# Transposes in row groups: a decoder layer's self attention on one NeuronCore

## The chip, the cores and the metric

The kernel runs on one core of one Trainium2 chip. The metric is the device time of one execution in microseconds (us), the median of several runs. The engines are called PE (TensorE; its weight loads are listed apart, as PEld), DVE (VectorE), ACT (ScalarE), POOL (GpSimd) and SP (SyncE, which issues the DMAs).

## The reference

One encoder layer over a short context (2 sequences of 77 rows) and one decoder layer over 2 sequences of T = 2048 rows, D = 512 wide, H = 16 heads of 32, all in float32. Cut to its core:

```python
def _mha(xq, xkv, w_in, b_in, w_out, b_out, bias):
    ...
    scores = jnp.einsum('bhqd,bhkd->bhqk', q, k) / jnp.sqrt(jnp.asarray(hd, xq.dtype))
    attn = jax.nn.softmax(scores + bias[None], axis=-1)
    out = jnp.einsum('bhqk,bhkd->bhqd', attn, v)
    return out.transpose(0, 2, 1, 3).reshape(Bq, Tq, D) @ w_out.T + b_out
...
x = x + _mha(_ln(x, ...), _ln(x, ...), enc_in_w, ...)          # encoder
memory = x + (relu(_ln(x, ...) @ enc_ff1_w.T + enc_ff1_b) @ enc_ff2_w.T + enc_ff2_b)
yn = _ln(y, dec_n1_s, dec_n1_b)
y = y + _mha(yn, yn, dec_sa_in_w, ..., sb)                     # causal, with a table of biases
y = y + _mha(_ln(y, ...), memory, dec_ca_in_w, ..., cb)
y = y + (relu(_ln(y, ...) @ dec_ff1_w.T + dec_ff1_b) @ dec_ff2_w.T + dec_ff2_b)
```

## The kernel before

**Stages.** The rows of x are cut into blocks of 512: two sequences b, four blocks m each. First comes self attention for all eight blocks; the small encoder runs in its first block, and the cross attention of the first block (`first_cross`) in the gaps of the second sequence. Then a second phase does cross attention and the feed-forward layer of each block, with products of halves and quarters (L1323, L1352, L1424) after Strassen's scheme.

**Self attention.** A unit is 128 query rows (t) of a block and a head group g of four heads: 128 units, each with i+1 = 4m+t+1 chunks of 128 keys. `pieces` cuts the chunks into pieces of one to four (kn). For each piece `scores` makes four matmuls, one for each head r, of 32 rows each on the four row groups of PE, into four PSUM banks (L376). DVE moves them to `pp` with their maxima (L385; the last 256 columns of a unit are added to the bias on the way, L392), and makes the negative maximum once the unit's scores are all there (L402). ACT makes the exponentials (L407), four a unit, put into the program bit by bit by `exps`.

`turn` takes one or two pieces, transposes the probabilities chunk by chunk and head by head (128 x 128, L428), four to a bank, and copies each filled bank to `pts` (L434 on ACT, L432 on DVE). For m = 0 the copies alternate between the engines; else the first half of the loads goes to ACT and the second to DVE. `values` then multiplies `pts` by the values, four heads side by side in columns, into bank 7 (L445).

**Order.** It is written out by hand (a manual schedule): every engine runs its instructions in the order in which the Python code emits them. The loop at the end takes one or two pieces of a unit and emits `turn`, then, after the unit's last piece, `slot` (a projection q, k, v or out, L215, L226, L239, L251; the turning of a normed row tile in `norm_turn`, L308; the division by the sums in `divide`, L464), one group of scores if `may_score` allows it, the values, and further scores. With m = 3 each unit has two turns of two pieces, of which the second has the projection; with m = 2 one of two pieces and one of one; with m = 1 one of two; with m = 0 one of one piece.

**Banks.** In self attention `bank()` hands out seven PSUM banks in a ring: four for a group of scores, one for each load of four transposes, one for a projection. In the second phase the ring has four. The buffer `pts` has room for 32 transposed tiles of 128 x 128, as many as a turn of two whole pieces makes.

**Second phase.** `norm_stages` turns a normed tile with four transposes into one bank (L759) and four activations. `attend_stages` turns the probabilities over the 77 context rows, four heads to a bank (L814), and copies each with ACT (L815).

Of the kernel before, what the change touches and what calls it, by code (L numbers as in the profile page):

```python
# [11 lines left out]
AF = mybir.ActivationFunctionType  # L12
ALU = mybir.AluOpType
# [41 lines left out]
def tile_encoder_decoder(ctx: ExitStack, tc: tile.TileContext, ins, out):  # L55
    nc = tc.nc
    x, src = ins["x"], ins["ctx_1024"]
# [10 lines left out]
    ident = const.tile([P, P], F32, name="ident")  # L68
# [89 lines left out]
    with (  # L158
# [6 lines left out]
        kT = ac.tile([P, NC, T], F32, name="kT")  # L165
# [28 lines left out]
        nTs, qTs, ots, sums_of = {}, {}, {}, {}  # L194
        wbig, xs, xr = {}, {}, {}
# [102 lines left out]
        def norm_turn(b, m, t, apart=False):  # L298
            xn = xs.pop((b, m, t))
            if t == 0:  # L300
                nTs[b, m] = nTt
            nT = nTs[b, m]

            pts = [bank()] * NC
            if apart:
                pts[0] = bank()
            for c in range(NC):
                nc.tensor.transpose(pts[c][:, ts(c, P)], xn[:, ts(c, P)], ident)  # L308
            for c in range(NC):
                d, pt = nT[:, c, ts(t, P)], pts[c]  # L310
                sc, bi = vec("dec_n1_s", c), vec("dec_n1_b", c)
                if c or not apart:
                    nc.scalar.activation(d, pt[:, ts(c, P)], AF.Identity, bias=bi, scale=sc)  # L313
                else:
                    nc.vector.tensor_scalar(d, pt[:, ts(c, P)], sc, bi, ALU.mult, ALU.add)


        def pieces(i):
# [94 lines left out]
        def turn(pieces):  # L413

            first = units[pieces[0][0]][1] == 0
            by_head = first or units[pieces[0][0]][2:] == (0, 0)
            loads = []
            for n, k0, kn in pieces:
                ks = range(k0, k0 + kn)
                if by_head:  # L420
                    loads += [[(n, k, r) for k in ks] for r in range(HC)]
                else:
                    loads += [[(n, k, r) for r in range(HC)] for k in ks]
            for o, load in enumerate(loads):
                pt = bank()
                pts = in_turn("pts", pts_all).rearrange("p (x q) -> p x q", q=P)
                for x, (n, k, r) in enumerate(load):
                    nc.tensor.transpose(pt[:, ts(x, P)], state[n]["p"][r][:, ts(k, P)], ident)  # L428
                    got[n, k, r] = pts[:, x, :]
                w = len(load) * P  # L430
                if o % 2 if first else o >= (len(loads) + 1) // 2:
                    nc.vector.tensor_copy(pts[:, : len(load), :], pt[:, :w])  # L432
                else:
                    nc.scalar.copy(pts[:, : len(load), :], pt[:, :w])  # L434
                if o == min(3, len(loads) - 1):
                    exps(1)
            exps(HC if first else 1)

# [14 lines left out]
        def divide(b, m, g):  # L453


            ri = sm.tile([P, TB, HC], F32, name="ri", tag="ri", bufs=2)
            nc.vector.reciprocal(ri, sums_of[b, m, g])
            rows = sm.tile([P, TB, HC, HD], F32, name="rirows", tag="rirows", bufs=1)
            nc.vector.tensor_copy(rows, ri[:, :, :, None].to_broadcast([P, TB, HC, HD]))
            yield  # L460
            rb = bank()
            flat = rows.rearrange("p t r d -> p (t r d)")
            for t in range(TB):
                nc.tensor.transpose(rb[:, ts(t, P)], flat[:, ts(t, P)], ident)  # L464
            nc.vector.tensor_tensor(ots[b, m, g], rb, ots[b, m, g], ALU.mult)
            yield


# [266 lines left out]
        def norm_stages(y, n, row, place, done):  # L735

            keep = {}

            def stats():
                st = sm.tile([P, 6], F32, name="bnst", tag="bnst")  # L740
                mv = sm.tile([P, 2], F32, name="cmv", tag="cmv", bufs=4)
                rs = sm.tile([P, 3], F32, name="crs", tag="crs", bufs=4)
                nc.vector.bn_stats(st, y())
                nc.vector.bn_aggr(mv, st)
                nc.vector.tensor_scalar_add(rs[:, 0:1], mv[:, 1:2], EPS)
                nc.gpsimd.tensor_tensor(rs[:, 1:2], rs[:, 0:1], mhalf[:, 0:1], ALU.pow)
                nc.gpsimd.tensor_scalar(rs[:, 2:3], mv[:, 0:1], rs[:, 1:2], -1.0, ALU.mult, ALU.mult)
                keep.update(rs=rs)

            def center():  # L750
                xn = keep["xn"] = place()
                rs = keep["rs"]
                nc.scalar.activation(xn, y(), AF.Identity, bias=rs[:, 2:3], scale=rs[:, 1:2])
                nc.gpsimd.tensor_tensor(y(), y(), row, ALU.add)

            def turned():
                xn, pt, dst = keep["xn"], bank(), done()
                for c in range(NC):
                    nc.tensor.transpose(pt[:, ts(c, P)], xn[:, ts(c, P)], ident)  # L759
                for c in range(NC):  # L760
                    sc, bi = vec(f"dec_{n}_s", c), vec(f"dec_{n}_b", c)
                    nc.scalar.activation(dst[:, c, :], pt[:, ts(c, P)], AF.Identity, bias=bi, scale=sc)

            return stats, center, turned

# [6 lines left out]
        def attend_stages(q, kTc, v, y, biased, pr, pts, place, w_o, bi=None):  # L772


            prh = pr.rearrange("p (h k) -> p h k", k=S)
# [32 lines left out]
                nc.gpsimd.tensor_tensor(prh, prh, ri[:, :, None].to_broadcast([P, H, S]), ALU.mult)  # L808

            def turned():  # L810
                for g in range(NC):
                    pt = bank()
                    for r in range(HC):
                        nc.tensor.transpose(pt[:S, ts(r, P)], prh[:, g * HC + r, :], ident)  # L814
                    nc.scalar.copy(pts(g), pt[:S, :])  # L815

            def times_v():
                ot = bank()
                for g in range(NC):
                    for r in range(HC):  # L820
                        h = g * HC + r
                        nc.tensor.matmul(  # L822
                            ot[rows4(r), ts(g, P)], v[:, ts(h, HD)], pts(g)[:, ts(r, P)], start=True, stop=True
                        )
                keep["oT"] = place()
                nc.scalar.copy(keep["oT"], ot)
# [9 lines left out]
        def first_cross():  # L836
# [21 lines left out]
            def pts(g):  # L858
                return kT[:S, g, 2 * MB : 3 * MB]

            def loads():
                for t in range(TB):
# [581 lines left out]
        def cross(x):  # L1444
# [26 lines left out]
            for t in range(TB):  # L1471
                at = 14 + 7 * t
                y = lambda t=t: y_of(x, t)
                biased = m == 0 and t < 2
                fs = attend_stages(
                    lambda g, t=t: qT[g // 2][:, g % 2, ts(t, P)], kTcs[b], vcs[b][:S, :], y, biased, pr,
                    lambda g: pts_all[:S, g, :], place("xr"), wbt,
                    bias_1 if biased and t else None,
                )
# [35 lines left out]
        i = 0  # L1515
# [93 lines left out]
```

## Time and profile before

| | |
|---|---|
| Median of 3 runs | 2827.0 us (2826.58 to 2828.27) |
| Span of the profiled execution | 2828.5 us |
| PE busy | 2796.6 us, 99% |
| DVE, ACT, POOL busy | 66%, 51%, 28% |
| Transposes of probabilities, L428 | 4352, busy 536.6 us |
| Their copies | 556 on DVE (L432), 330.8 us; 598 on ACT (L434), 298.8 us |
| Scores, L376 | 2560 instructions (two passes each), busy 356.6 us |
| Values, L445 | 8704 instructions (two passes each), busy 278.8 us |

The profile is of one execution; its span and the median agree within 1.5 us. An engine's busy time is the time in which at least one of its instructions ran, so instructions that overlap count once; the mean is that of one instruction from its start to its end, with the time in the pipeline. The chain of waits starts at the last instruction and goes back, at each step, to what released it. In the views, "<-" after an idle time names what ended it.

### The profile page before, as it was taken

Reading aid. Unit: us, or ns where it says so; the run is one execution under the profiler, and the core shown is the slowest. Engines: PE = TensorE matmul, PEld = TensorE weight load, DVE = VectorE, ACT = ScalarE, POOL = GpSimd, SP = SyncE. Lnnn points to the kernel's source line nnn. Section 1 sums busy time; section 2 is a strip of 40 time slices with the busy share of each in tenths; the row PEclk is TensorE's granted clock in tenths of the full one; section 3 lists DMA queues with packets and bytes.
Section 4 is the critical chain, followed back from the end, with each engine's and each line's share of the span. In section 5 each row is a group of like instructions: output and inputs, shape, how many; then the busy total and the mean of one; then the engine's idle time right before and its main releaser. Section 6 shows DMA issues by size and latency. Waiting matters only on the chain.

```text
span 2828.5 us, 65166 instructions
## 1 busy us (share of the span) xinstructions
PE 2796.6 (99%) x25950; PEld 2062.6 (73%) x25950; DVE 1872.9 (66%) x5288; ACT 1454.0 (51%) x2785; POOL 787.9 (28%) x697
## 2 busy tenths in 40 slices
PE   9899999999999999999999999999999999999998
PEld 5557666666666556666666677888888888888888
DVE  4666687778887577687878895464645555555545
ACT  3544466656666556656656676434344444444431
POOL 0200050200000201120100002282828283837356
PEclk9999999999999999999999999999999999999999
DMA  6414343401111412332401014463637464646466
GB/s 172 122 33 130 119 137 103 125 17 46 34 44 58 120 48 61 80 102 68 124 20 32 21 60 144 135 216 116 205 120 207 138 197 127 194 131 187 125 201 194
DMA packets 252642, 319.10 MB, mean 113 GB/s; under 512 B 29568, under 2 KB 142512, under 8 KB 252210
## 3 DMA queue, kind: packets, MB, share of 16 engines
q1 hardware_dynamic: 252338, 314.93, 37.7%
q8 instruction: 205, 3.36, 0.5%
q14 instruction: 99, 0.81, 0.1%
HBM read 274.91 MB, written 39.95 MB: 111 GB/s over the span
## 4 chain that ended last, share of the span: by engine, by line
PE 93%; DVE 3%; ACT 1%; issue 1%; DMA 1%; POOL 1%; SPq 0%; POOLq 0%; ACTq 0%; DVEq 0%
PE psum L428 17%; PE psum L1323 14%; PE psum L1352 12%; PE psum L376 11%; PE psum L445 9%; PE psum L215 4%; PE psum L831 4%; PE psum L251 4%; PE psum L239 4%; PE psum L226 3%; PE psum L1424 3%; PE psum L814 2%; DVE pp L385 1%; PE psum L784 1%; PE psum L822 1%; PE psum L546 1%
## 5 line engine op out<-in xcount | busy, mean ns | idle before, releaser
L407 ACT ACTIVATE pp<-pp,nm 128x128 f32<-128x128 f32 (+15 forms) x512 | 612.7, 1204 | 219.7 <-DVE nm L402 219.2
L385 DVE TENSOR_SCALAR_CACHE_REDUCE pp<-psum 128x512 f32<-128x512 f32 (+3 forms) x1024 | 559.4, 591 | 61.7 <-PE psum L376 60.2
L428 PEld LDWEIGHTS psum<-ident,pp 128*128 128x128 f32 x4352 | 472.9, 141 | 111.8 <-DVE pp L385 53.1
L428 PE MATMUL psum<-ident,pp 128*128 128x128 f32 x4352 | 536.6, 277 | 9.2 <-ACT pp L407 2.8
L434 ACT COPY pts<-psum 128x512 f32<-128x512 f32 (+3 forms) x598 | 298.8, 571 | 437.6 <-PE psum L428 333.4
L432 DVE COPY pts<-psum 128x512 f32<-128x512 f32 (+3 forms) x556 | 330.8, 648 | 68.6 <-PE psum L428 68.5
L376 PE MATMUL psum<-kT,q 32*128 32x512 f32 (+3 forms) x2560 | 356.6, 576 | 6.0 <-ACT nT L313 2.7
L445 PEld LDWEIGHTS psum<-pts,vv 128*32 128x32 f32 x8704 | 226.0, 110 | 123.9 <-issue 116.0
L1352 PEld LDWEIGHTS psum<-pp 128*128 128x128 f32 x2560 | 295.8, 192 | 17.4 <-issue 12.8
L1352 PE MATMUL psum<-pp 128*128 128x128 f32 x2560 | 306.4, 276 | 1.9 <-POOL pp L1105 1.6
L445 PE MATMUL psum<-pts,vv 128*32 128x128 f32 x8704 | 278.8, 275 | 0.7 <-ACT pts L434 0.5
L1105 POOL TENSOR_TENSOR pp<-pp 128x512 f32<-128x512 f32 x155 | 209.5, 1368 | 111.7 <-DMA pp<-in_dec_ff_wT_dram 90.8
L1323 PE MATMUL psum<-vv,pp 128*128 128x256 f32 x1024 | 238.5, 381 | 0.0
L376 PEld LDWEIGHTS psum<-kT,q 32*128 32x128 f32 x2560 | 122.9, 183 | 141.2 <-issue 87.9
L1323 PEld LDWEIGHTS psum<-vv,pp 128*128 128x128 f32 x1024 | 189.8, 190 | 26.3 <-issue 1.9
L392 DVE CUSTOM_DVE_ANT_0 pp<-psum,bias 128x256 f32<-128x256 f32 (+1 forms) x512 | 196.0, 411 | 17.0 <-PE psum L376 17.0
L285 POOL TENSOR_TENSOR rstd<-rstd,mhalf 128x1 f32<-128x1 f32 x32 | 18.2, 569 | 659.1 <-DVE rstd L284 608.6
L1336 DVE TENSOR_TENSOR kT<-kT,psum 128x512 f32<-128x512 f32 x96 | 65.7, 685 | 181.0 <-PE psum L1323 181.0
L1339 ACT ACTIVATE kT<-kT,vecs 128x256 f32<-128x256 f32 x192 | 86.9, 500 | 168.7 <-DVE kT L1336 168.1
L1323 PE MATMUL psum<-nT,pp 128*128 128x256 f32 x768 | 173.4, 379 | 0.0
L1323 PEld LDWEIGHTS psum<-nT,pp 128*128 128x128 f32 x768 | 145.3, 190 | 22.6 <-issue 3.5
L808 POOL TENSOR_TENSOR oT<-oT,cri 128x1232 f32<-128x1232 f32 x28 | 67.7, 2416 | 283.4 <-DVE cri L803 258.4
(193 smaller groups left out, 3724.5 us busy)
## 6 DMA issues: line engine op xcount, KB each, us to landing
pp<-w_d SPq DMA_DIRECT2D x520, 256.0 KB, 2.9
pp<-in_dec_ff_wT_dram SPq DMA_DIRECT2D x112, 256.0 KB, 4.0
wqk<-in_dec_sa_in_wT_dram SPq DMA_DIRECT2D x64, 256.0 KB, 4.0
bias<-tzg SPq DMA_DIRECT2D x128, 128.0 KB, 3.8
wbig<-in_dec_sa_in_wT_dram SPq DMA_DIRECT2D x8, 1024.0 KB, 6.4
vv<-in_enc_ff_wT_dram SPq DMA_DIRECT2D x8, 1024.0 KB, 5.2
wbig<-in_dec_sa_out_wT_dram SPq DMA_DIRECT2D x8, 1024.0 KB, 6.4
vv<-y SPq DMA_DIRECT2D x32, 256.0 KB, 5.1
```

Source lines behind the costliest of these rows:

```text
L215: nc.tensor.matmul(mm, w[:, c, :], nTs[b, m][:, c, :], start=(c == 0), stop=(c == NC - 1))
L376: nc.tensor.matmul(banks[r][:, : kn * P], q[rows4(r), ts(t, P)], kT[rows4(r), g, k0 * P : (k0 + kn) * P], start=True, stop=True,)
L385: nc.vector.tensor_scalar(p[:, k0 * P : (k0 + far) * P], s[:, : far * P], 1.0, None, ALU.mult, ALU.max, accum_out=st["mx"][:, r, c : c + 1],)
L392: nc.vector.tensor_tensor_reduce(p[:, (i + 1) * P - w : (i + 1) * P], s[:, far * P : kn * P], biases[b, m, g][:, r, 2 * P - w :], 1.0, LOW ...
L407: nc.scalar.activation(p, p, AF.Exp, bias=nm, accum_out=to)
L428: nc.tensor.transpose(pt[:, ts(x, P)], state[n]["p"][r][:, ts(k, P)], ident)
L432: nc.vector.tensor_copy(pts[:, : len(load), :], pt[:, :w])
L434: nc.scalar.copy(pts[:, : len(load), :], pt[:, :w])
L445: nc.tensor.matmul(ot[rows4(r), t, :], vv[:, k, ts(g * HC + r, HD)], got.pop((n, k, r)), start=(k == 0), stop=(k == i),)
L1105: engine.tensor_tensor(out, a, b, ALU.subtract)
L1323: nc.tensor.matmul(mm[:, ts(f, TOK)], a[:, c, ts(f, P)], b[:, c, :], start=fresh and f == 0 and c == 0, stop=c == 1, skip_group_check=True,)
L1352: nc.tensor.matmul(psum[:, bank_i, ts(col, P)], lhs[:, c, :], w[:, c, :], start=fresh and k in (0, 3) and c == 0, stop=c == 3, skip_group_ ...
```

## The change

`turn` makes each 128 x 128 transpose in four parts: 32 query rows each, on the row group of those rows, and each row group writes to a bank of its own. So a piece of kn chunks fills four banks together, each with w = 4 kn strips of 32 columns, and then has four copies: banks 0 and 2 by DVE, 1 and 3 by ACT, in this order of emission DVE, ACT, DVE, ACT. A copy writes runs of 32 columns, 128 apart. `pts` is handed out by tiles instead of by loads of four. The exp that stood after a turn's fourth load stands after its first piece.

The other transposes of 128 rows (`norm_turn`, `divide`, `turned` in `norm_stages` and in `attend_stages`) are made in two parts of 64 rows, into two banks (`two_banks`, `turn_halves`); the instruction that empties them reads both banks at once, or, in `attend_stages`, copies eight heads' strips of one bank for two head groups at a time.

The diff, cut to its core:

```diff
+HALF = P // 2
...
+        pts_ring = pts_all.rearrange("p s (x q) -> p (s x) q", q=P)
...
+        def two_banks():
+            n = count["bank"]
+            count["bank"] += 2
+            i, j = sorted((n % count["banks"], (n + 1) % count["banks"]))
+            return psum[:, i : j + 1 : j - i, :]
+
+        def turn_halves(pt, x, src, width=P):
+            for a in range(2):
+                rows = slice(a * HALF, (a + 1) * HALF)
+                nc.tensor.transpose(pt[:width, a, ts(x, HALF)], src[rows], ident[rows, rows])
+
+        def joined(t):
+            return t.rearrange("p (a q) -> p a q", a=2)
...
-            pts = [bank()] * NC
+            pts = [two_banks()] * NC
...
-                nc.tensor.transpose(pts[c][:, ts(c, P)], xn[:, ts(c, P)], ident)
+                turn_halves(pts[c], c, xn[:, ts(c, P)])
...
         def turn(pieces):
             first = units[pieces[0][0]][1] == 0
-            by_head = first or units[pieces[0][0]][2:] == (0, 0)
-            loads = []
-            for n, k0, kn in pieces:
+            if count["pts"] + sum(HC * kn for _, _, kn in pieces) > pts_ring.shape[1]:
+                count["pts"] = 0
+            for o, (n, k0, kn) in enumerate(pieces):
                 ks = range(k0, k0 + kn)
...
-            for o, load in enumerate(loads):
-                pt = bank()
-                pts = in_turn("pts", pts_all).rearrange("p (x q) -> p x q", q=P)
-                for x, (n, k, r) in enumerate(load):
-                    nc.tensor.transpose(pt[:, ts(x, P)], state[n]["p"][r][:, ts(k, P)], ident)
+                first_unit = first or units[n][2:] == (0, 0)
+                load = [(k, r) for r in range(HC) for k in ks] if first_unit else [(k, r) for k in ks for r in range(HC)]
+                w = len(load)
+                pt = [bank() for _ in range(HC)]
+                pts = pts_ring[:, count["pts"] : count["pts"] + w, :]
+                count["pts"] += w
+                for x, (k, r) in enumerate(load):
+                    for a in range(HC):
+                        rows = rows4(a)
+                        nc.tensor.transpose(
+                            pt[a][:, ts(x, HD)], state[n]["p"][r][rows, ts(k, P)], ident[rows, rows]
+                        )
                     got[n, k, r] = pts[:, x, :]
-                w = len(load) * P
-                if o % 2 if first else o >= (len(loads) + 1) // 2:
-                    nc.vector.tensor_copy(pts[:, : len(load), :], pt[:, :w])
-                else:
-                    nc.scalar.copy(pts[:, : len(load), :], pt[:, :w])
-                if o == min(3, len(loads) - 1):
+                for a in range(HC):
+                    (nc.scalar.copy if a % 2 else nc.vector.tensor_copy)(
+                        pts[:, :, ts(a, HD)], pt[a][:, : w * HD].rearrange("p (x q) -> p x q", q=HD)
+                    )
+                if o == 0:
                     exps(1)
             exps(HC if first else 1)
...
             def turned():
-                for g in range(NC):
-                    pt = bank()
-                    for r in range(HC):
-                        nc.tensor.transpose(pt[:S, ts(r, P)], prh[:, g * HC + r, :], ident)
-                    nc.scalar.copy(pts(g), pt[:S, :])
+                for g in range(0, NC, 2):
+                    pt = two_banks()
+                    for x in range(2 * HC):
+                        turn_halves(pt, x, prh[:, g * HC + x, :], S)
+                    d = pts.rearrange("p g (r a q) -> p g r a q", r=HC, a=2)[:, g : g + 2]
+                    for a in range(2):
+                        nc.scalar.copy(
+                            d[:, :, :, a, :], pt[:S, a, :].rearrange("p (g r q) -> p g r q", g=2, q=HALF)
+                        )
```

More of the change, by code (lines that the diff above doesn't have):

```diff
@@ L302, in norm_turn @@
             nT = nTs[b, m]
-            pts = [bank()] * NC
+            pts = [two_banks()] * NC
             if apart:
-                pts[0] = bank()
+                pts[0] = two_banks()
             for c in range(NC):
-                nc.tensor.transpose(pts[c][:, ts(c, P)], xn[:, ts(c, P)], ident)
+                turn_halves(pts[c], c, xn[:, ts(c, P)])
             for c in range(NC):
-                d, pt = nT[:, c, ts(t, P)], pts[c]
+                d, pt = joined(nT[:, c, ts(t, P)]), pts[c][:, :, ts(c, HALF)]
                 sc, bi = vec("dec_n1_s", c), vec("dec_n1_b", c)
                 if c or not apart:
-                    nc.scalar.activation(d, pt[:, ts(c, P)], AF.Identity, bias=bi, scale=sc)
+                    nc.scalar.activation(d, pt, AF.Identity, bias=bi, scale=sc)
                 else:
-                    nc.vector.tensor_scalar(d, pt[:, ts(c, P)], sc, bi, ALU.mult, ALU.add)
+                    nc.vector.tensor_scalar(d, pt, sc, bi, ALU.mult, ALU.add)
         def pieces(i):
@@ L460, in divide @@
             yield
-            rb = bank()
+            rb = two_banks()
             flat = rows.rearrange("p t r d -> p (t r d)")
             for t in range(TB):
-                nc.tensor.transpose(rb[:, ts(t, P)], flat[:, ts(t, P)], ident)
-            nc.vector.tensor_tensor(ots[b, m, g], rb, ots[b, m, g], ALU.mult)
+                turn_halves(rb, t, flat[:, ts(t, P)])
+            o = ots[b, m, g].rearrange("p (t a q) -> p a t q", t=TB, a=2)
+            nc.vector.tensor_tensor(
+                o, rb[:, :, : TB * HALF].rearrange("p a (t q) -> p a t q", q=HALF), o, ALU.mult
+            )
             yield
@@ L756, in turned @@
             def turned():
-                xn, pt, dst = keep["xn"], bank(), done()
+                xn, pt, dst = keep["xn"], two_banks(), done()
                 for c in range(NC):
-                    nc.tensor.transpose(pt[:, ts(c, P)], xn[:, ts(c, P)], ident)
+                    turn_halves(pt, c, xn[:, ts(c, P)])
                 for c in range(NC):
                     sc, bi = vec(f"dec_{n}_s", c), vec(f"dec_{n}_b", c)
-                    nc.scalar.activation(dst[:, c, :], pt[:, ts(c, P)], AF.Identity, bias=bi, scale=sc)
+                    nc.scalar.activation(
+                        joined(dst[:, c, :]), pt[:, :, ts(c, HALF)], AF.Identity, bias=bi, scale=sc
+                    )
             return stats, center, turned
@@ L810, in turned @@
             def turned():
-                for g in range(NC):
-                    pt = bank()
-                    for r in range(HC):
-                        nc.tensor.transpose(pt[:S, ts(r, P)], prh[:, g * HC + r, :], ident)
-                    nc.scalar.copy(pts(g), pt[:S, :])
+                for g in range(0, NC, 2):
[6 more added lines that the diff above has]
+                            d[:, :, :, a, :], pt[:S, a, :].rearrange("p (g r q) -> p g r q", g=2, q=HALF)
+                        )
             def times_v():
@@ L822, in times_v @@
                         nc.tensor.matmul(
-                            ot[rows4(r), ts(g, P)], v[:, ts(h, HD)], pts(g)[:, ts(r, P)], start=True, stop=True
+                            ot[rows4(r), ts(g, P)], v[:, ts(h, HD)], pts[:, g, ts(r, P)], start=True, stop=True
                         )
@@ L856, in first_cross @@
             oT, xn = kT[:, 1, 3 * MB :], kT[:, 2, 3 * MB :]
-            def pts(g):
-                return kT[:S, g, 2 * MB : 3 * MB]
+            pts = kT[:S, :, 2 * MB : 3 * MB]
             def loads():
@@ L1476, in cross @@
                     lambda g, t=t: qT[g // 2][:, g % 2, ts(t, P)], kTcs[b], vcs[b][:S, :], y, biased, pr,
-                    lambda g: pts_all[:S, g, :], place("xr"), wbt,
+                    pts_all[:S, :NC, :], place("xr"), wbt,
                     bias_1 if biased and t else None,
```

4 lines of the change are left out of this document (removed).

## The prediction

> **What bounds the kernel now.** I read first the page's list of busy time, then the busy time by window, one window for each query block of the two sequences, cut at the times at which the blocks' first transposes start.
>
> ```profile
> span 2828.5 us, 65166 instructions
> ...
> PE 2796.6 (99%) x25950; PEld 2062.6 (73%) x25950; DVE 1872.9 (66%) x5288; ACT 1454.0 (51%) x2785; POOL 787.9 (28%) x697
> ```
> ```profile
> 622.20:904.40 282.20, 280.44 (x3421) 193.39 (x3417) 232.69 (x729) 185.30 (x275) 8.17 (x12) 1.00 0.13 39
> 904.40:1044.50 140.10, 136.59 (x933) 73.85 (x929) 86.66 (x325) 74.10 (x214) 18.74 (x25) 0.98 0.37 99
> 1044.50:1239.60 195.10, 194.52 (x1971) 122.72 (x1970) 145.47 (x483) 122.24 (x245) 33.47 (x35) 1.00 0.27 77
> 1239.60:1473.90 234.30, 233.37 (x2553) 154.37 (x2553) 183.43 (x588) 144.71 (x236) 23.19 (x24) 1.00 0.24 73
> 1850.00:2828.00 978.00, 970.45 (x7362) 849.20 (x7356) 522.95 (x922) 382.61 (x816) 558.01 (x454) 1.00 0.56 168
> ```
>
> After the window's length each row has PE, weight loads, DVE, ACT and POOL. PE is full everywhere, but DVE is not far behind where the blocks are long: 233 of 282 us for the fourth block (m=3), 183 of 234 for m=2. So a faster PE stage meets DVE soon, and what matters is who waits for whom inside one turn. The chain of waits shows a turn of m=3 without and then one with a projection, and one with a wait in it (start, length, what):
>
> ```profile
> 701.21 3.64 PE psum L428 x32
> 704.85 1.07 PE psum L376 x8
> 705.92 1.89 PE psum L445 x64
> 707.81 1.07 PE psum L376 x8
> 708.88 2.33 PE psum L428 x20
> 711.21 0.44 PE psum L464 x4
> 711.65 3.54 PE psum L215 x8
> ```
> ```profile
> 726.20 2.77 PE psum L428 x24
> ...
> 735.03 1.07 PE psum L376 x8
> 736.10 2.89 PE psum L428 x24
> 738.98 0.03 issue
> 739.01 1.09 PE psum L428 x8
> ```
>
> A turn is: transposes of two pieces (L428), perhaps a projection (L215), one group of scores (L376), values (L445), another group of scores. From 24 against 20 transposes, one is 0.44/4 = 0.11 us, and entering them after scores costs 2.77 - 24 x 0.11 = 0.13. The two turns last 7.67 (701.21 to 708.88) and about 9.5 us, all PE work. The timeline of DVE has the reductions that empty the score banks and the copies of the transposes:
>
> ```profile
> 701.75 0.42 DVE L392 CUSTOM_DVE_ANT_0 pp<-psum,bias 128x256 f32<-128x256 f32 x1
> ...
> 703.24 0.17 DVE L402 TENSOR_REDUCE nm<-mx 128x4 f32<-128x16 f32 x1
> 703.58 2.48 DVE L432 COPY pts<-psum 128x512 f32<-128x512 f32 x4 [0.17 <-PE psum L428]
> ```
> ```profile
> 734.21 0.69 DVE L385 TENSOR_SCALAR_CACHE_REDUCE pp<-psum 128x512 f32<-128x512 f32 x1
> ...
> 734.82 0.69 DVE L385 TENSOR_SCALAR_CACHE_REDUCE pp<-psum 128x512 f32<-128x512 f32 x1
> ...
> 736.12 0.42 DVE L385 TENSOR_SCALAR_CACHE_REDUCE pp<-psum 128x256 f32<-128x256 f32 x1
> ...
> 738.53 0.42 DVE L392 CUSTOM_DVE_ANT_0 pp<-psum,bias 128x256 f32<-128x256 f32 x1
> ...
> 738.99 0.17 DVE L402 TENSOR_REDUCE nm<-mx 128x4 f32<-128x20 f32 x1
> 739.09 2.47 DVE L432 COPY pts<-psum 128x512 f32<-128x512 f32 x4
> ```
>
> Call D the time in which DVE empties the last group of scores before a turn: 4 x 0.61 = 2.45 us for 512 columns (734.21 to 734.82 is one), 1.66 for a closing piece of 256 (701.75 to 703.41), 2.97 for a closing one of 512 (736.12 to 739.09); about 2.45 for a closing one of 384. A copy is 2.48/4 = 0.62 and starts 0.17 after PE; PE went on at 739.01, 0.06 after the last reduction that it needed (738.53 + 0.42). Note that the transposes start at once after the scores (736.10) although DVE has all of D before it: each load of four takes one bank, the first four are copied by ACT, and only the seventh meets a bank that DVE has yet to empty. That slack is what the change touches.
>
> **The change part by part.** *Speed of a quarter transpose.* It has no row; I build it.
>
> ```profile
> L428 PEld LDWEIGHTS psum<-ident,pp 128*128 128x128 f32 x4352 | 472.9, 141 | 111.8 <-DVE pp L385 53.1 <-issue 33.2 <-DVE mx L392 7.7
> L1352 PEld LDWEIGHTS psum<-pp 128*128 128x128 f32 x2560 | 295.8, 192 | 17.4 <-issue 12.8 <-POOL pp L1105 3.5 <-DVE pp L1105 0.5
> L445 PEld LDWEIGHTS psum<-pts,vv 128*32 128x32 f32 x8704 | 226.0, 110 | 123.9 <-issue 116.0 <-DVE pp L385 4.6 <-ACT pts L434 1.8
> L784 PEld LDWEIGHTS psum<-pts,bias 32*128 32x128 f32 x896 | 27.5, 186 | 7.8 <-issue 7.0
> L784 PE MATMUL psum<-pts,bias 32*128 32x77 f32 x896 | 31.7, 277 | 0.0
> ```
>
> A load of 32 columns lasts 110 ns, one of 128 192: 0.85 ns a column on a fixed 83. A transpose's load lasts 141, so it holds the array for about 58. The loads of L784 go to four row groups and last 186 each, yet 896 take 27.5 us, 31 ns apiece, so the groups work side by side. The moving side of a quarter is 32 columns, a quarter of 0.11 us, below its load. So four quarters cost about 0.06 us (estimate) against 0.11, all 4352 transposes 218 us less of PE if nothing else waited. Bounds: 0.03 (the moving side alone) and 0.14, four times the 35 ns apiece of the L784 matmuls; I take 0.06 since those have twice a transpose's load. The Trainium skill ("TensorE: Matmul & The Clock Gate", LDWEIGHTS) speaks against the change: a load's time goes by its columns, and one of 32 rows lasts as long as one of 128. The trace agrees (186 against 192 ns); side by side is then the only gain.
>
> *Banks.* All four banks of a piece are now filled at the same time, and two pieces take eight of a ring of seven. The first piece needs banks of the earlier scores and the first of the last ones; the second needs the other three of the last scores, and for its fourth bank the first piece's first bank, which DVE copies (a=0). In DVE's queue that copy stands behind all of D. So in every turn of two pieces PE stops, between them, until D and one copy are done. Behind the waiting transpose stand the projection, the scores and the values. From the end of the last scores to the end of the transposes: 0.17 + D + 0.62 + 0.06, then 0.1 of filling and 0.06 for each (k, head) of the second piece, whatever the first takes. With D = 2.45 and 16 of them that is 3.30 + 1.06 = 4.36, against 3.64.
>
> *Turns with a projection* add 0.2 on going back to whole-array matmuls (entry into scores now: 1.07 less two of 3.54/8). In m=3 the scores before are of 512: for 20, 24, 28, 32 transposes now 2.33, 2.77, 3.21, 3.64, then 4.08, 4.08, 4.32, 4.56: +1.75, +1.31, +1.11, +0.92, 5.1 for the four units of a head group. Seven of eight groups have projections: +36; the eighth about +7. In m=1 the D before are 1.66, 2.45, 2.97, 1.66: +0.96, +1.31, about +1.3 (DVE makes PE wait there today already), +0.13; 3.7 x 8 groups: +29.
>
> *Turns of m=3 without one.* The next scores' fourth bank is the second piece's first, copied by DVE: 0.17 + 0.62 + 0.06 = 0.85 more; 0.1 is saved as scores follow transposes in the same row mode. With D = 1.66, 2.45, 2.97, 1.66: 4.32, 5.11, 5.63, 4.32 against 3.64, 3.83, 4.01, 3.64 (4.01 is 2.89 + 0.03 + 1.09): +4.3 a group, +34 for eight. So m=3 gets 77 us longer, some 14%.
>
> *m=2* alternates: a turn of two pieces loses 0.1 to 1.2 (values stand between its scores and two of them, and hide part of D), a turn of one piece has no second to wait and gains 0.05 a transpose less 0.2: +2.8 and -1.85 a group, +8 in all. *m=0* has one piece a turn: -11 by the same rule, -8 taken, since PE already idles there (136.6 of 140.1).
>
> *Halves.* These have the rows
>
> ```profile
> L759 PE MATMUL psum<-ident,xt 128*128 128x128 f32 x152 | 23.0, 274 | 0.0
> L814 PE MATMUL psum<-ident,oT 128*77 128x128 f32 x448 | 53.9, 274 | 0.0
> L308 PE MATMUL psum<-ident,xt 128*128 128x128 f32 x120 | 18.5, 277 | 1.2 <-DVE xt L296 1.0
> ```
> A pair of halves takes 0.06 by the same load. L759's 64 stages and L308's 32 go from 4 x 0.11 to 0.24, but stand between whole-array products, and pay both entries, 0.13 + 0.19: +0.12 a stage, +12 with L464's. L814's 32 stages go from 16 x 0.12 = 1.92 to 0.96 + 0.32: -20. Together about -5, PE being the bound there; -45 if these entries cost nothing, +38 if halves don't run side by side. The Trainium skill ("TensorEngine Tiling (Array Packing)", Key Properties) says that changing the mode drains the array; the 0.13 and 0.19 agree, and no row shows it for 64 rows.
>
> *At no cost:* the number of 512-wide copies and DVE's share stay about as they are (480 on DVE before), and the new destination runs of 32 columns are taken to copy as fast. If not, each 0.1 us of a copy costs some 20 us over the 128 turns of two pieces. ACT's copies of the second piece stand behind an exp, and still end before the values. No DMA is added or moved, but PE's program grows by some 14,000 pairs of load and matmul, and so do its fetches:
>
> ```profile
> q8 instruction: 205, 3.36, 0.5%
> ```
> They use little of the DMA engines; if they fall behind in a burst, it gets longer, which the upper end covers.
>
> Sum: 77 + 29 + 8 - 8 - 5 = +101 on 2828.5, so 2929.5; the median is 1.5 lower: **2928 us**.
>
> **The rivals.** *Faster, near 2620:* the PE saving is collected, 218 us less some entries, with DVE's 233 us as the floor of m=3. It decides the other way only if the first piece's copy is done when the first piece is: D + 0.85 below about 1.1. The smallest D is 1.66, so I see no turn where it holds. For it speaks the full PE. A weaker form is no change: with quarters at 0.03 and halves without entries, 2 x 50 us come off and the sum is about zero, 2820 to 2835.
> *Quarters no faster, 3050:* their load is as long as a matmul's, 0.11 for four. Then the second pieces (and the single ones) cost 0.05 more for each (k, head): 44 + 104 + 108 + 40 of them a group for m=1, 2, 3, 0, times 8 is 2368, +123. For it: L784's 35 ns apiece. Against it: 141 against 192 ns.
> *The change doesn't do what it says:* the groups go one after the other, four loads of 58 ns, 0.23 for a transpose against 0.11: 4352 x 0.12 = +520, near 3350. The L784 loads speak against it.
>
> **How the numbers follow.** My forecast 0.72 (its own range 2875 to 2990), quarters no faster 0.13, serial 0.04, faster 0.06, no change or little 0.05. The range is 2860 to 3060. About 0.2% is what a measurement tells from no change: faster 0.07, same 0.03, slower 0.90.
>
> **What would show it.** In the profile after: transposes in m=3 come in two bursts with a stop of 1.5 to 2.5 us between, put down to DVE's copy of the transposes; about 0.06 us for four within a burst; no-projection turns near 9.1 instead of 7.7 us; m=3 windows near 320 us, m=2 hardly changed, m=0 slightly shorter; PE busy well below 99% and DVE idle before the copies. Wrong would be an m=3 window at or below 282, or a second piece that follows the first at once.

## The result and the profile after

| | before | after |
|---|---|---|
| median | 2827.64 us (2826.58 to 2829.27, 4 runs) | 3328.31 us (3323.79 to 3334.65, 4 runs) |
| profiled execution | 2828.5 us | 3323.7 us |
| ratio | | 1.1775, 95% interval 1.1759 to 1.1792 |

The change makes the kernel slower by 17.8%, five times the loss that was forecast. The page's first lines, and its rows for the transposes (L448) and their copies by DVE (L453):

```profile
span 3323.7 us, 93651 instructions
...
PE 3040.7 (91%) x40030; PEld 2106.4 (63%) x40030; DVE 1904.2 (57%) x5372; ACT 1451.6 (44%) x2827; POOL 786.1 (24%) x697
...
PEclk9888888887777799888888777779999999999999
...
L448 PE MATMUL psum<-ident,pp 32*128 32x32 f32 x17408 | 462.4, 234 | 209.4 <-DVE pts L453 78.7
L448 PEld LDWEIGHTS psum<-ident,pp 32*128 32x128 f32 x17408 | 391.0, 149 | 335.4 <-DVE pp L404 124.1
...
L453 DVE COPY pts<-psum 128x512 f32<-128x512 f32 (+3 forms) x640 | 359.8, 604 | 134.9 <-PE psum L448 93.0
```

Two things are new. PE stands idle before transposes, 209 us in all against 9 before, and waits there for DVE: 79 us for its copies (L453), 67 and 53 for the reductions ahead of them (L404, L411). And the row of granted clock, all nines before, has sevens and eights through most of self attention. By window, cut at the blocks' first transposes as before (the last five columns are POOL, its count, granted clock, DMA share, GB/s):

```profile
35.90:186.00 150.10, 134.44 (x1538) 75.12 (x1537) 89.64 (x337) 66.05 (x195) 19.54 (x20) 0.90 0.40 106
186.00:455.00 269.00, 236.30 (x3285) 152.27 (x3281) 147.96 (x509) 104.53 (x219) 26.93 (x28) 0.87 0.30 93
455.00:748.50 293.50, 264.10 (x4604) 160.74 (x4604) 188.12 (x602) 146.10 (x244) 44.99 (x45) 0.84 0.25 74
748.50:1155.90 407.40, 348.85 (x6240) 216.41 (x6236) 239.83 (x743) 183.75 (x279) 8.19 (x12) 0.76 0.09 28
1155.90:1306.40 150.50, 137.04 (x1477) 70.64 (x1473) 86.17 (x325) 74.23 (x214) 18.72 (x25) 0.93 0.34 92
1306.40:1553.80 247.40, 215.65 (x3317) 126.79 (x3312) 150.65 (x497) 121.13 (x253) 33.43 (x35) 0.86 0.22 66
1553.80:1847.70 293.90, 268.04 (x4605) 161.47 (x4604) 187.71 (x602) 146.01 (x244) 23.21 (x24) 0.83 0.18 55
1847.70:2227.00 379.30, 324.43 (x6091) 205.51 (x6088) 230.38 (x707) 170.27 (x246) 7.61 (x6) 0.77 0.11 34
2227.00:3323.70 1096.70, 1081.95 (x8793) 919.13 (x8789) 571.50 (x1011) 431.27 (x914) 598.94 (x490) 1.00 0.54 166
```

The fourth block (m=3) takes 407 us instead of 282, in the second sequence 379 instead of 266, and even m=2, hardly changed in the forecast, 294 instead of 234. The clock that was granted there is 0.76 to 0.84 of full. The trace records it as switching between full and half, in steps of 3.41 us. What that does is seen in a turn of m=3 (timeline; the number in brackets is the idle time before, and what ended it):

```profile
872.39 0.93 PE L448 MATMUL psum<-ident,pp 32*128 32x32 f32 x46 [0.82 <-DVE pp L404]
...
874.09 1.02 DVE L453 COPY pts<-psum 128x384 f32<-128x384 f32 x2
...
874.70 0.89 PE L448 MATMUL psum<-ident,pp 32*128 32x32 f32 x29 [0.22 <-DVE pts L453]
...
877.16 0.34 PEld L234 LDWEIGHTS psum<-nT,wqk 128*128 128x128 f32 x1 [0.52 <-issue]
878.01 0.34 PEld L234 LDWEIGHTS psum<-nT,wqk 128*128 128x128 f32 x1 [0.52 <-issue]
878.63 0.19 PEld L234 LDWEIGHTS psum<-nT,wqk 128*128 128x128 f32 x1 [0.28 <-issue]
879.06 0.19 PEld L234 LDWEIGHTS psum<-nT,wqk 128*128 128x128 f32 x1 [0.24 <-issue]
879.49 0.19 PEld L234 LDWEIGHTS psum<-nT,wqk 128*128 128x128 f32 x1 [0.24 <-issue]
```

This turn has pieces of 48 and 32 quarters. The row of 46 ends at 873.3 with the first piece; the last 29 of the second can start only at 874.70, once DVE has made the first of its two copies (874.09): this is the stop between the pieces that was forecast. The projection after it (L234) begins at half clock: its loads stand 0.85 us apart and last 0.34, and from 879 on they stand 0.43 apart and last 0.19.

How much is the clock? A window of length L and granted clock c has 2(1-c)L of half clock, in which PE does no less than half its work, so at most (1-c)L is lost: 0.10 x 150 + 0.13 x 269 + 0.16 x 294 + 0.24 x 407 + 0.07 x 151 + 0.14 x 247 + 0.17 x 294 + 0.23 x 379 = 377 us, against some 8 before. Of the 495 us between the two profiled executions, up to 370 are thus the clock; at least 125 are left for all that the prediction had in its sum (+101).

### The profile page after: what moved, and what is told of

Same layout as the page of the kernel before. It is cut to its first block, busy times and chain, and to the rows that moved or that the text cites. A ratio compares the mean times of both kernels' runs of the same rounds, so it can differ in the third digit from the quotient of the medians.

```text
span 3323.7 us, 93651 instructions
## 1 busy us (share of the span) xinstructions
PE 3040.7 (91%) x40030; PEld 2106.4 (63%) x40030; DVE 1904.2 (57%) x5372; ACT 1451.6 (44%) x2827; POOL 786.1 (24%) x697
## 5 line engine op out<-in xcount | busy, mean ns | idle before, releaser
L453 ACT COPY pts<-psum 128x512 f32<-128x512 f32 (+3 forms) x640 | 301.8, 524 | 935.3 <-PE psum L448 868.6
L404 DVE TENSOR_SCALAR_CACHE_REDUCE pp<-psum 128x512 f32<-128x512 f32 (+3 forms) x1024 | 560.1, 591 | 236.1 <-PE psum L395 234.7
L448 PE MATMUL psum<-ident,pp 32*128 32x32 f32 x17408 | 462.4, 234 | 209.4 <-DVE pts L453 78.7
L448 PEld LDWEIGHTS psum<-ident,pp 32*128 32x128 f32 x17408 | 391.0, 149 | 335.4 <-DVE pp L404 124.1
L395 PE MATMUL psum<-kT,q 32*128 32x512 f32 (+3 forms) x2560 | 458.9, 655 | 9.7 <-DVE pp L404 3.4
L453 DVE COPY pts<-psum 128x512 f32<-128x512 f32 (+3 forms) x640 | 359.8, 604 | 134.9 <-PE psum L448 93.0
L466 PEld LDWEIGHTS psum<-pts,vv 128*32 128x32 f32 x8704 | 297.6, 136 | 176.5 <-issue 156.9
L466 PE MATMUL psum<-pts,vv 128*32 128x128 f32 x8704 | 370.5, 334 | 4.1 <-issue 2.3
L395 PEld LDWEIGHTS psum<-kT,q 32*128 32x128 f32 x2560 | 158.9, 211 | 169.2 <-issue 104.1
L411 DVE CUSTOM_DVE_ANT_0 pp<-psum,bias 128x256 f32<-128x256 f32 (+1 forms) x512 | 196.0, 411 | 22.7 <-PE psum L395 20.3
L270 PE MATMUL psum<-wbig,oT 128*128 128x512 f32 x256 | 156.0, 766 | 18.3 <-ACT nT L332 10.7
```

What stands on the lines that cost most here:

```text
L270: nc.tensor.matmul(mm, ots[b, m, c][:, ts(t, P)], w[:, c, :], start=(c == 0), stop=(c == NC - 1))
L395: nc.tensor.matmul(banks[r][:, : kn * P], q[rows4(r), ts(t, P)], kT[rows4(r), g, k0 * P : (k0 + kn) * P], start=True, stop=True,)
L404: nc.vector.tensor_scalar(p[:, k0 * P : (k0 + far) * P], s[:, : far * P], 1.0, None, ALU.mult, ALU.max, accum_out=st["mx"][:, r, c : c + 1],)
L411: nc.vector.tensor_tensor_reduce(p[:, (i + 1) * P - w : (i + 1) * P], s[:, far * P : kn * P], biases[b, m, g][:, r, 2 * P - w :], 1.0, LOW ...
L448: nc.tensor.transpose(pt[a][:, ts(x, HD)], state[n]["p"][r][rows, ts(k, P)], ident[rows, rows])
L453: (nc.scalar.copy if a % 2 else nc.vector.tensor_copy)(pts[:, :, ts(a, HD)], pt[a][:, : w * HD].rearrange("p (x q) -> p x q", q=HD))
```

## The experiments

A time without an interval is of one run.

**What brings the clock down.** Theory A: it is granted by how much of the array works. A whole transpose uses 128 x 128 cells while 128 columns pass; its four quarters use 32 x 128 cells for 32 columns each, a quarter as much in all. Theory B: it falls because PE waits, whatever it does between. Theory C: the waits alone are longer than worked out, and the clock is no matter.

*full_dealt* puts whole transposes back, but deals them round the four banks of a piece, with the copies as in the change, so that the waits stay.

```diff
-                    for a in range(HC):
-                        rows = rows4(a)
-                        nc.tensor.transpose(
-                            pt[a][:, ts(x, HD)], state[n]["p"][r][rows, ts(k, P)], ident[rows, rows]
-                        )
+                    nc.tensor.transpose(pt[x % HC][:, ts(x // HC, P)], state[n]["p"][r][:, ts(k, P)], ident)
...
-                        pts[:, :, ts(a, HD)], pt[a][:, : w * HD].rearrange("p (x q) -> p x q", q=HD)
+                        pts[:, a::HC, :], pt[a][:, : kn * P].rearrange("p (x q) -> p x q", q=P)
```

> Whole 128 x 128 transposes again, but dealt round the four banks of a piece, with the copies of the changed kernel (DVE, ACT, DVE, ACT, after the whole piece): the waits of the change without its row groups. Theory A (the clock is granted by how much of the array works, and a quarter transpose uses a quarter of what a whole one uses): clock back to 0.97 or more in the m=3 windows, span near 3020 us (2928 and 0.05 us for each of the 1700 transposes of second pieces). Theory B (the clock falls because PE waits, whatever it does in between): clock near 0.77 in m=3 as in the changed kernel, span 3300 or more.

3094.1 us, with m=3 (window of the first sequence):

```profile
701.80:1041.40 339.60, 309.45 (x3452) 201.43 (x3448) 240.46 (x743) 184.93 (x283) 8.19 (x12) 0.97 0.11 33
```

PE is busy for 309 of 340 us, so it waits for 9%, and the clock is 0.97. Waits of this size alone don't bring it down; they are shorter than in the changed kernel, though (99 us before transposes in the whole run, against 209). The time is 74 us above what A gave; it is still 234 us below the changed kernel although its transposes are slower.

*fill_full* and *fill_quarter* keep the quarters and put idle matmuls into the waits, whole-array ones in the first and ones of 32 rows in the second; the bank is written over afterwards. Each run has one of the two marked lines.

```diff
                 w = len(load)
...
+                if not first:
+                    for _ in range(7 if o else 3):
+                        nc.tensor.matmul(pt[0][:, :P], ident, ident, start=True, stop=True)      # fill_full
+                        nc.tensor.matmul(pt[0][:, :P], ident[:HD], ident[:HD], start=True, stop=True)  # fill_quarter
                 for x, (k, r) in enumerate(load):
```

> The changed kernel, and for m above 0 some idle matmuls of the whole array on the identity, into a bank that is written afterwards: 3 (two passes of 0.11 us each) before a first piece, 7 before a second, where PE waits for DVE. Both A and B: the clock is back near 1.0 in m=3, and the span falls to 2920 to 2980 us, what the waits cost at full clock. If the clock is not what the time went to (theory C, the waits are longer than I worked out), the span stays above 3250.

> As the run with idle matmuls of the whole array, but these have 32 rows: the same number, the same columns, a quarter of the array. A: the clock in m=3 stays below 0.9 and the span above 3100 us. B: as good as the whole array, 2920 to 2980 us.

3160.2 us and 3361.2 us. The windows of m=3, first fill_full, then fill_quarter:

```profile
725.30:1073.50 348.20, 338.85 (x6867) 237.55 (x6866) 238.08 (x741) 185.35 (x281) 8.20 (x12) 1.00 0.11 33
```
```profile
791.80:1171.20 379.40, 363.85 (x6872) 260.87 (x6871) 239.15 (x741) 185.32 (x281) 8.17 (x12) 0.87 0.10 30
```

The two differ in the rows of the idle matmuls alone. Both keep PE busy for 96 to 97% of the window, and yet one has the clock at 1.00 and the other at 0.87 (0.80 in the second sequence). So it is the use of the array that counts, not the time in which PE is busy: A. (The rows differ here; whether the columns count as well wasn't tried apart.) And more work made the kernel faster by 168 us, so C falls: at least a third of the loss is the clock. The fill_full time is 180 us above what I expected; the idle matmuls also delay real ones. Turns of one piece, which have 3 of them, look the likeliest: the second block of m=2, which has such turns, takes 278 us here and 267 in the next run, which leaves these out.

*fill_second* has 5 idle matmuls, before second pieces only.

```diff
+                if o:
+                    for _ in range(5):
+                        nc.tensor.matmul(pt[0][:, :P], ident, ident, start=True, stop=True)
                 for x, (k, r) in enumerate(load):
```

> The changed kernel with idle matmuls of the whole array before second pieces only, 5 instead of 3 and 7 (m=0 and turns of one piece have none). A (the array's use sets the clock): the clock in m=3 is 0.93 or more, and the span lies at or below the 3158 us of 3 and 7, between 3060 and 3160, since fewer idle matmuls delay real ones. If the wait itself were what is left, not the clock, the span would go back towards 3250 or more.

3128.4 us, and m=3

```profile
715.40:1064.70 349.30, 315.97 (x6556) 214.34 (x6552) 239.06 (x743) 185.35 (x283) 8.19 (x12) 0.95 0.11 33
```

as A has it. At this clock a window loses at most 0.05 x 349 = 17 us, so m=3 would take about 332 us at full clock, and 312 in the second sequence (318 at 0.98): 320 and 304 were forecast (282 and 266, and half of 77).

**What the wait for DVE's copy costs.** *copies_by_piece* gives the first piece's copies to ACT and the second's to DVE.

```diff
-                    (nc.scalar.copy if a % 2 else nc.vector.tensor_copy)(
+                    (nc.scalar.copy if (a % 2 if len(pieces) == 1 else o == 0) else nc.vector.tensor_copy)(
```

> The changed kernel with the four copies of a first piece on ACT and of a second on DVE (alternating only where a turn has one piece): the second piece no longer waits for a copy that stands behind the reductions, only for these. By my wait theory each of the 128 turns of two pieces gets 0.6 us shorter at full clock, 80 us, and double that at half clock: 3170 to 3260 us. A: the clock stays below 0.9 in m=3. If the copy behind the reductions is not what PE waits for, the time stays within 1% of the changed kernel.

3251.2 us, 77 below the changed kernel, with

```profile
746.60:1124.20 377.60, 331.06 (x6236) 211.36 (x6232) 233.42 (x743) 186.39 (x281) 8.17 (x12) 0.79 0.10 30
```

The copy behind the reductions is a cost, of the size expected (the view of waits is shown below), and the clock stays down, since the quarters use as little of the array as before. Over the whole span 0.887 is granted, against 0.883 in the changed kernel; by the sum above that is some 22 of the 77 us. The gain is not even: the blocks of m=1 and m=3 get 15 to 30 us shorter, and those of m=2 longer, 308 and 297 us instead of 294 and 294. Why is open.

*copies_fill* has both edits, copies by piece and 5 idle matmuls before second pieces.

> The two cures together: copies by piece, and 5 idle matmuls of the whole array before second pieces. At full clock the wait of the second piece for DVE's copy alone is then taken out: 0.6 us for each of 128 turns against the run with 5 idle matmuls (3128 us), so 3030 to 3070 us, with the clock in m=3 at 0.93 or more. If the copy behind the reductions weren't a cost at full clock, 3110 or more.

3127.4 us: a miss, nothing gained on 3128.4. The blocks differ: m=3 of the first sequence takes 340 us instead of 349 and m=1 of the second 221 instead of 233, but the two of m=2 take 284 and 275 instead of 273 and 267. The timeline of a turn of m=3 shows what the two cures do to each other (L447 are the idle matmuls, L451 the second piece):

```profile
1744.93 1.38 PE L447 MATMUL psum<-ident 128*128 128x128 f32 x10
...
1746.24 1.19 PE L451 MATMUL psum<-ident,pp 32*128 32x32 f32 x64
...
1747.46 2.48 DVE L456 COPY pts<-psum 128x512 f32<-128x512 f32 x4 [1.82 <-PE psum L451]
```

The idle matmuls now stand in the wait's place, DVE idles for 1.82 us, and all four copies of the second piece follow one another on DVE for 2.48 us, where two on each engine took 1.3. How much of the gain that eats, and why m=2 loses, is open: this run doesn't tell what the wait costs at full clock; that stays with the turns below.

**The halves.** *only_halves* is the kernel before with the changed `norm_turn`, `divide` and both `turned`; *turn_only* is the kernel before with the changed `turn`.

> The kernel before with only the transposes in two halves (norms, division by the sums, cross attention), the transposes of probabilities as before. By the terms of the prediction the span falls by 5 us or moves little. By the second phase of the changed kernel (1097 us against 1088) it rises by 10 to 20 us, to 2835 to 2850, with the clock at 1.0 as before.

> The changed transposes of probabilities alone, all others whole as before. If the halves cost 10 to 20 us, it is 3305 to 3320 us, with the clock in m=3 at 0.76 as in the changed kernel: the whole loss but for these. If the halves have a part in the fall of the clock, below 3280.

2871.65 us, ratio 1.015 (1.0133 to 1.0167), so +44 us; and 3267.75 us, 60 below the changed kernel. The halves cost 44 us alone and 60 on top of the changed `turn`, where 10 to 20 were expected, and not in one place. turn_only came out below the 3280 that were to show a part of the halves in the fall of the clock; it is a smaller part: over the span 0.886 is granted against 0.883, by the sum above some 17 of the 60 us. The stretch before the first transposes of probabilities, the first block and the second phase, in only_halves and then before:

```profile
0.00:35.90 35.90, 29.54 (x127) 18.34 (x128) 12.23 (x45) 8.24 (x22) 4.49 (x13) 0.86 0.60 150
35.90:185.00 149.10, 137.23 (x1058) 78.57 (x1056) 89.89 (x337) 66.37 (x195) 19.53 (x20) 0.93 0.39 104
1775.20:2870.50 1095.30, 1080.57 (x8787) 917.86 (x8785) 571.30 (x1012) 429.74 (x912) 598.31 (x490) 1.00 0.54 166
```
```profile
0.00:29.60 29.60, 25.49 (x110) 16.13 (x111) 12.13 (x45) 8.17 (x22) 4.49 (x13) 1.00 0.73 181
29.60:173.60 144.00, 134.76 (x1030) 76.84 (x1028) 89.72 (x337) 66.17 (x195) 19.56 (x20) 0.98 0.40 108
1740.20:2828.50 1088.30, 1080.25 (x8111) 937.61 (x8109) 573.58 (x1012) 429.00 (x912) 600.68 (x490) 1.00 0.56 167
```

They lose 6 us at the start, where four row tiles are turned one after the other, 5 in the first block (10 in the second sequence's), 7 in the second phase, and the rest in the blocks between. At the start and in the first blocks the clock is lower too (0.86 and 0.93 against 1.00 and 0.98). In the second phase it is waiting: PE is busy as long as before (1080.6 and 1080.3 us), in a window that is 7 us longer. Waits of this kind stand before the out projections (L251 before, L270 in only_halves, over the whole run; the last column is PE's idle time and what ended it):

```profile
L251 PE MATMUL psum<-wbig,oT 128*128 128x512 f32 x256 | 115.8, 595 | 0.0
```
```profile
L270 PE MATMUL psum<-wbig,oT 128*128 128x512 f32 x256 | 123.4, 627 | 10.8 <-ACT pp L784 7.5 <-ACT nT L332 2.7 <-DVE pp L404 0.6
```

PE waits there 11 us for ACT, which empties the banks of a turned row tile (L332, L784); in the changed kernel 18, in turn_only nothing.

**A version with both conditions kept.** If the loss comes from banks filled together and from an array too little used, row groups should pay where neither happens. *in_halves* transposes the probabilities in two halves of 64 rows, in loads of eight (k, head) with two banks each; the first half of a turn's copies goes to ACT, the second to DVE, so that no load needs a bank copied behind the reductions. All other transposes are whole.

```diff
+                loads += [load[i : i + 2 * HC] for i in range(0, len(load), 2 * HC)]
+            for o, load in enumerate(loads):
+                w = len(load)
+                pt = [bank(), bank()]
...
+                    for a in range(2):
+                        rows = slice(a * HALF, (a + 1) * HALF)
+                        nc.tensor.transpose(
+                            pt[a][:, ts(x, HALF)], state[n]["p"][r][rows, ts(k, P)], ident[rows, rows]
+                        )
...
+                    on_act = a == 0 if first else 2 * o + a < len(loads)
```

> The kernel before with the transposes of probabilities in two halves of 64 rows: loads of eight (k, head) that fill two banks, the first half of a turn's copies on ACT and the second on DVE, so that no load needs a bank which is copied behind the reductions. By the waits: a whole turn's transposes end 0.06 + 0.6 us after the last reduction at the latest, about as early as before; single pieces gain. A: half the array's use in transposes is left, enough for a clock of 0.95 or more in m=3: 2790 to 2870 us. If any transposes in row groups bring the clock down or the waits back: 2900 or more.

2813.95 us, ratio 0.9952 (0.9938 to 0.9967): 0.5% faster than the kernel before. m=0, 1 and 3 gain 2 to 5 us a block; m=2 loses 5 and 2:

```profile
381.40:620.50 239.10, 228.01 (x3225) 140.35 (x3224) 184.36 (x594) 144.59 (x235) 49.56 (x48) 0.95 0.32 91
...
1226.70:1463.30 236.60, 225.73 (x3227) 139.46 (x3226) 183.84 (x594) 144.63 (x235) 23.17 (x24) 0.96 0.24 73
```

The clock is at 0.95 there, and some second loads wait for an ACT copy:

```profile
487.70 0.71 PE L434 MATMUL psum<-ident,pp 64*128 64x64 f32 x15 [1.12 <-ACT pts L440]
```

*halves_mixed* therefore leaves m=2 with whole transposes in single banks (loads of four, one part instead of two).

```diff
+                step = HC if units[n][1] == 2 else 2 * HC
-                loads += [load[i : i + 2 * HC] for i in range(0, len(load), 2 * HC)]
+                loads += [load[i : i + step] for i in range(0, len(load), step)]
+            parts = 1 if units[pieces[0][0]][1] == 2 else 2
```

> The transposes of probabilities in halves for m=0, 1 and 3, whole ones in single banks for m=2, where the run in halves has the clock at 0.95 and a wait for ACT's copy, and takes 239 and 237 us instead of 234 and 234. If the clock and that wait are what m=2 lost: the m=2 windows go back to 234 and the clock there to 1.0, the rest stays, about 2806 us, 7 us below the run in halves and 0.7% below the kernel before. If m=0 and m=1 gain only because the halves of m=2 come before them (the clock or the order carries over), less.

2809.17 us, the median of five, ratio 0.9931 (0.9918 to 0.9945), and m=2 is as it was before:

```profile
383.40:617.90 234.50, 233.51 (x2554) 154.51 (x2554) 183.25 (x586) 144.60 (x235) 49.67 (x48) 1.00 0.33 92
```

## Why the prediction was wrong

**The direction and the wait were right.** The second piece of a turn stops for DVE's copy of the first, as the order of the ring said, and copies_by_piece got 77 us back by moving that copy. In the changed kernel's view of waits (us, times, longest) it stands as

```profile
PE psum L448 <- DVE pts L453: 78.7, 128, 1.6
```

once in each of the 128 turns of two pieces, 0.61 us each; the forecast had 0.62 for it. In m=3 it is 1.0 to 2.6 us from the start of the first piece's last quarter to the start of the second's fourth, 1.5 in the middle; 1.5 to 2.5 were forecast. At full clock the turns have about the length that was worked out, or somewhat more. In fill_second, whose clock is nearly full, the four kinds of turn of m=3 without a projection typically take 9.5, 9.5, 9.7 and 9.0 us from first transpose to first transpose (7.7 to 8.0 before); the terms of the sum give 8.4, 9.1, 9.7 and 8.4. Those with a projection take 11.0 to 11.7; the forecast was 9.46 + 1.75, 9.9 + 1.31, 9.87 + 1.11 and 10.73 + 0.92, so 11.0 to 11.7. The idle matmuls stand in these turns, and by an estimate from DVE's copies in that trace up to half a us of a turn is theirs.

**The speed of a quarter was right.** In fill_full a piece of 64 quarters takes

```profile
1791.10 1.19 PE L451 MATMUL psum<-ident,pp 32*128 32x32 f32 x64
```

1.19 us from the start of the first to the end of the last; less the 0.22 that one lasts, the 64 starts lie within 0.97 us, so that four take 0.06. At half clock four take 0.107. The rival in which the groups go one after the other gave a time near the measured one (3350) for a reason that is plainly wrong; a rival whose number comes true isn't shown by that. (In the rival before it, 2368 times 0.05 is 118, not 123; nothing hangs on it.)

**The step that failed** is the one that isn't there: the clock was put at no cost without a reason. Every duration in the sum was one of before, at a granted clock of 0.98 to 1.00, and the list of what comes at no cost doesn't have the clock. The prediction even said that PE would be busy well below 99%, and 218 us less of PE work was its own number; it never asked what clock such a PE is granted. It was 0.76 to 0.93 in the blocks. That is up to 370 of the 495 us by the sum over the windows, and at least 200 by fill_second, which has more work and a clock of 0.965. m=3 came to 407 and 379 us instead of 320 and 304 mostly for that reason: at full clock fill_second puts it at 332 and 312.

**m=2 and m=1.** The forecast has +8 us for both blocks of m=2 and +29 for both of m=1; the windows grew by 119 (294 + 294 - 234 - 234) and 107 (269 + 247 - 214 - 195). At clocks of 0.83 to 0.87 the loss to the clock is at most 97 and 70 of these, so at least some 20 and 40 are left for waits and halves: more than the terms in both.

**The halves** were a term of -5 and measured +44. The range given for them in the text, -45 to +38, doesn't hold it. L814's stages gained as worked out (1024 halves busy for 42.6 us, 36.9 and 5.7, against 61.6 whole). What was missing were PE's waits for ACT, which the term had put at nothing: at the start, where halves put four banks of seven under each row tile (3.5 us in one wait), and before the out projections (11 us); and the clock of the first blocks (0.93 and 0.95, some 12 us more than before by the sum over windows). The prediction priced the entries and the loads of these halves, and not the second bank that each takes. With the changed `turn` such a wait costs more: in fill_second two out projections of m=3 wait 2.3 and 2.5 us for ACT and then run at half clock, and their turns take 17.3 and 18.5 us instead of 10.3 and 11.2 in the kernel before.

## What to carry to other kernels

Before making PE's work lighter, ask what share of the array it uses in each few microseconds, not only how long PE is busy; a transpose cut into row groups is quicker and can still halve the clock of the matmuls around it. Splitting an output over banks that fill together takes away the overlap that single banks give: find the first bank that must come round again, the engine that frees it, and what stands ahead of that in its queue. In this kernel two row groups, in loads of two banks, gained 0.5%, and 0.7% where m=2 kept whole transposes; four, with the halves elsewhere, lost 17.8%.

## What the runs showed of the hardware

**The clock goes by the array's use.** For each step of 3.41 us of self attention at full clock I added up, over the matmuls that start in it, active rows x active columns x columns moved x 0.83 ns (a projection's passes of 512 columns start 0.43 us apart), and divided by 128 x 128 x 3.41 us. Steps before a fall to half clock have 0.06 to 0.43 in the trace after (124 of them, median 0.26), 0.11 to 0.34 in that of before (3), and 0.08 to 0.44 in that of in_halves (18). Steps that kept the clock have 0.41 or more before, and in the trace after 0.38 or more in 95 of 100. So the line lies near 0.4 of the array in these traces, with some steps on its wrong side. The share of PE's busy time doesn't tell the two apart: fill_quarter is at 96% and 0.87. Of the 446 steps at full clock in its self attention, the best line of busy time has 91 on the wrong side, the best line of array use 30.

The Trainium skill ("TensorE: Matmul & The Clock Gate", Part 1) names two states of the clock, full and half, set by how busy PE was in a free-running window of 3413 ns, and gives the rule of no idle gap of PE above about 3.4 us. The steps of 3.41 us and the half agree. That rule alone would not have warned here: in m=3 of the changed kernel PE is busy 86% of the time, and the waits before its transposes in the first sequence are 1.4 us long at most by the view of waits:

```profile
PE psum L448 <- DVE pts L453: 19.6, 32, 1.4
PE psum L448 <- DVE pp L404: 19.5, 37, 0.8
```

**Row groups work side by side in transposes too.** Four quarters in 0.06 us and two halves in 0.062 to 0.069, against 0.109 for a whole one: the trace of before showed this only for matmuls.
